# A fused Perceiver layer in f32: transposes among products, one more product ahead, another bank for the counts, and the last rows in two banks

## The chip, the core and the metric

The kernel runs on one core of a Trainium2 chip. The metric is the device time of one execution in microseconds (us), as the median of several runs. A profiled execution gives a trace beside it: every instruction of every engine with its start and its duration.

## What is computed

A tensor `x` of 8 x 64 rows of 512 numbers passes three blocks, each added to `x`, all in f32:

```
x = x + xattn(layernorm(x), ctx_1024, W, b)      # cross attention: 8 x 1601 context rows
x = x + attn(layernorm(x), wq, wk, wv, wo, ...)  # causal linear attention, 16 heads of 64, then an MLP with gelu
x = x + ffn(layernorm(x), w_router, w0, w1, wo)  # 8 experts, top 2 per row, gated by softmax
```

- `xattn`: scores of each row against all context rows, softmax, weighted sum, times `W`, relu.
- `attn`: its own layernorm, `q` and `k` through `elu(. @ proj) + 1`, `v = h @ wv`, running sums over the rows, `@ wo`, then layernorm and a hidden layer of 2048.
- `ffn`: the router picks two of eight experts for each row; each expert is `(silu(x @ w0) * (x @ w1)) @ wo`, and the two results are added with their weights.

## The kernel before

The 512 rows are four tiles of 128 (`NT = 4`), and the 512 features four chunks of 128 (`KC = 4`). All engines but the DMA queues run in the order in which the code is written. Loads of the context and of all weights come in one fixed order through a ring of twelve 1 MB buffers (`stream`, `need`), issued on SyncE's queue.

PSUM has eight banks of 512 columns. Up to the experts two rings of four are used: `mm_bank` for short results, and `acc_bank` for those that accumulate longer (or lie apart for another reason). For the experts both rings are closed (`banks.close()`) and a new pool `pse` is opened over the same eight banks, with `side_bank` (three for the whole tiles, two for the small groups) and `y_bank` (one bank for each of 0, 1 and "w"). A bank that comes around again, or that a pool takes over, makes its first writer wait for the readers of what lay there. Two engines that read one bank are put one after the other too: the second waits on a semaphore of the first.

The four places of the change, in the order of time:

1. Cross attention, around 160 to 178 us. The loop over tiles makes the attended rows of a tile (`attended`), and VectorE and ScalarE turn them into `hn` (`add_and_normalize`: two layernorms). `turn_h(t)` transposes `hn` on TensorE (line 552) and VectorE scales the four pieces into `h_t` (line 554). `values(t, n)` multiplies `h_t` of tile t with half n of `wv` (line 567), four products into one bank. After the loop stand the products of tile 2, the transposes of tile 3, and the products of tile 3.
2. The output projection of linear attention, around 252 to 290 us. `output(t, js)` adds the products of tile t for the pairs of heads j in `js` (line 758). The last pair, j = 7, comes from `attend_j(7)`: two groups of products (lines 712, 722), then on VectorE an addition (731), a reciprocal (732) and a product into `a_t` (734). Products for other j stand ahead of those that need j = 7. Then `join(t)` adds the result to `xin` and takes its statistics, `normal(t)` normalizes it, and `turn_h2(t)` transposes it for the MLP; the first hidden products (`hidden`, line 839) need these.
3. The border between routing and experts, around 403 to 410 us. `first_rows` gathers the rows of the first expert by products with one-hot matrices into two banks; ScalarE copies the one and VectorE the other into `xg_t0` (line 1110). One product with ones gives the experts' counts of rows (line 1107), and VectorE copies them (line 1112). The first expert's products (`up`, line 1243) read `xg_t0`.
4. The end, from 615 us. The last expert's tile, key (7, 0), goes through `whole_tile`: four `up` products into hidden quarters, each gated, transposed (`hidden_t`, line 1208), and multiplied by `down(q, h_t)` (line 1251) into one bank `y`. `add_rows` scales `y` by the gate, for this tile half on ScalarE (line 1218) and half on VectorE (line 1219), and GpSimd writes the rows to `out` by an indirect DMA that adds (line 1224).

Of the kernel before, what the change touches and what calls it, by code (L numbers as in the profile page):

```python
# [16 lines left out]
AF = mybir.ActivationFunctionType  # L17
# [16 lines left out]
NQ = 4  # L34
# [13 lines left out]
def perceiver_kernel(  # L48
# [35 lines left out]
    def mm_bank(name):  # L84
        return ps.tile([P, 512], F32, tag="mm", name=name)

    def acc_bank(name):
        return ps.tile([P, 512], F32, tag="acc", name=name)
# [460 lines left out]
    def turn_h(t):  # L549
        bank = mm_bank(f"tr_h_{t}")  # L550
        for c in range(KC):
            nc.tensor.transpose(bank[:, c * P : (c + 1) * P], hns[t][:, c * P : (c + 1) * P], ident)
        for c in range(KC):
            nc.vector.tensor_scalar(  # L554
                h_t[:, c, t * P : (t + 1) * P],
                bank[:, c * P : (c + 1) * P],
                g1_c[:, c : c + 1],
                beta1_c[:, c : c + 1],
                ALU.mult,
                ALU.add,  # L560
            )

    def values(t, n):
        wv_n = need("wv", n)
        bank = mm_bank(f"v_{n}_{t}")
        for c in range(KC):
            nc.tensor.matmul(  # L567
                bank, h_t[:, c, t * P : (t + 1) * P], wv_n[:, c, :], start=(c == 0), stop=(c == KC - 1)
            )
        nc.scalar.copy(v_sb[:, t, n * 512 : (n + 1) * 512], bank)  # L570
# [49 lines left out]
            values(t - 2, 1)  # L620
        attended(t)
    add_and_normalize(NT - 1)
    for n in range(2):
        values(NT - 2, n)
    turn_h(NT - 1)
    for n in range(2):
        values(NT - 1, n)
    done(("wv", 0), ("wv", 1))
# [6 lines left out]
    if True:  # L635
# [118 lines left out]
        def output(t, js):  # L754
            if t not in wo_banks:
                wo_banks[t] = (mm_bank if t < 2 else acc_bank)(f"wo_{t}")
            for j in js:
                nc.tensor.matmul(  # L758
                    wo_banks[t],
                    a_t[:, j, t * P : (t + 1) * P],  # L760
                    wo_r[j // 4][:, j % 4, :],
                    start=(j == 0),
                    stop=(j == nj - 1),
                )
# [8 lines left out]
        products(nj - 1)  # L773
        output(1, range(nj - 2))
        attend_j(nj - 1)
        output(2, range(nj // 2))
        for t in range(2):
            output(t, [nj - 2, nj - 1])

# [34 lines left out]
        of = join(0), join(1)  # L814
        for t in range(2):
            normal(t, *of[t])
        output(2, range(nj // 2, nj))
        of = join(2)
        output(3, range(nj // 2))
        normal(2, *of)  # L820
# [282 lines left out]
    count_tile(t)  # L1103
    first_rows(KC)

    bank = mm_bank("counts")
    nc.tensor.matmul(bank[:, :NE], ones, members[:, NT - 1, :], start=True, stop=True)
    xg_t0 = [moe.tile([P, 2, P], F32, name=f"xgT_first_{h}") for h in range(2)]
    for h, copy in enumerate([nc.scalar.copy, nc.vector.tensor_copy]):
# [31 lines left out]
    if True:  # L1141
# [5 lines left out]
        def y_bank(side, name):  # L1147
            return pse.tile([P, 512], F32, tag=f"y{side}", name=name)
# [64 lines left out]
        def add_rows(key, y, n, side, by_vector=False):  # L1213

            _, dst, gate = slots[key]
            y_sb = moe2.tile([P, D], F32, tag=f"ysb{side}", bufs=2 - side, name=f"y_sb_{key[0]}_{key[1]}")
            if key == (NE - 1, 0):
                nc.scalar.activation(y_sb[:n, : D // 2], y[:n, : D // 2], AF.Copy, scale=gate[:n, :])
                nc.vector.tensor_scalar(y_sb[:n, D // 2 :], y[:n, D // 2 :], gate[:n, :], None, ALU.mult)
            elif by_vector:  # L1220
                nc.vector.tensor_scalar(y_sb[:n, :], y[:n, :], gate[:n, :], None, ALU.mult)
            else:
                nc.scalar.activation(y_sb[:n, :], y[:n, :], AF.Copy, scale=gate[:n, :])  # L1223
            nc.gpsimd.indirect_dma_start(  # L1224
                out=out,
                out_offset=bass.IndirectOffsetOnAxis(ap=dst[:n, :], axis=0),
                in_=y_sb[:n, :],
                in_offset=None,
                bounds_check=B * S + P - 1,
                oob_is_err=True,  # L1230
                compute_op=ALU.add,
            )

        def whole_tile(key, up_of, down_of, between=lambda k: None, side=0):


            nm = f"{key[0]}_{key[1]}"
            xg_t = turned[key]

            def up(q):  # L1240
                bank = side_bank(side, f"up_{nm}_{q}")
                for c in range(KC):
                    nc.tensor.matmul(  # L1243
                        bank, xg_t[c], up_of[q][:, c, :], start=(c == 0), stop=(c == KC - 1)
                    )
                return gated(side, bank, f"{nm}_{q}")

            def down(q, h_t):
                w = down_of[q // 2]
                for j in range(2):  # L1250
                    nc.tensor.matmul(  # L1251
                        y, h_t[:, j, :], w[:, 2 * (q % 2) + j, :], start=(q + j == 0), stop=(q + j == NQ)
                    )

            hid0 = up(0)
            hid1 = up(1)
            h_t0 = hidden_t(side, hid0, f"{nm}_0")
            hid2 = up(2)
            y = y_bank(side, f"y_{nm}")
            down(0, h_t0)  # L1260
            h_t1 = hidden_t(side, hid1, f"{nm}_1")
            between(0)
            hid3 = up(3)
            h_t2 = hidden_t(side, hid2, f"{nm}_2")
            down(1, h_t1)
            between(1)
            h_t3 = hidden_t(side, hid3, f"{nm}_3")
            down(2, h_t2)
            between(2)
            down(3, h_t3)  # L1270
            add_rows(key, y, P, side)

        def group(e, up_of, down_of):


            nm = f"{e}_1"
            xg_t = turned[e, 1]


            split = "p (w n) -> p w n"  # L1280
            halves = [slice(h * P, (h + 1) * P) for h in range(2)]
            hid, h_t = [], {}

            def turn(j):
                bank = side_bank(1, f"ht_{nm}_{j}")
                nc.tensor.transpose(bank[:, :P], hid[j], ident)
                h_t[j] = moe2.tile([P, P], F32, tag="hidT1", name=f"hidT_{nm}_{j}")
                (nc.scalar.copy if j else nc.vector.tensor_copy)(h_t[j], bank[:, :P])

            for h in range(2):  # L1290

                bank = side_bank(1, f"up_{nm}_1") if h else y_bank(1, f"up_{nm}_0")
                for c in range(KC):

                    if h == 1 and c == KC - 1:
                        turn(0)
                    for q in range(NQ):
                        nc.tensor.matmul(
                            bank[q * R : (q + 1) * R, : 2 * P].rearrange(split, w=2),
                            xg_t[c],  # L1300
                            up_of[q][:, c, :].rearrange(split, w=2)[:, :, halves[h]],
                            start=(c == 0),
                            stop=(c == KC - 1),
                        )
                act = moe2.tile([P, P], F32, tag="act1", name=f"act_{nm}_{h}")
                nc.scalar.activation(act, bank[:, :P], AF.Silu)
                hid.append(moe2.tile([P, P], F32, tag="mid1", name=f"mid_{nm}_{h}"))
                nc.vector.tensor_tensor(hid[h], bank[:, P : 2 * P], act, ALU.mult)
            sums = {}

            def down(j, n):
                if j == 0:
                    sums[n] = y_bank(1, f"yq_{nm}_1") if n else side_bank(1, f"yq_{nm}_0")
                for q in range(NQ):
                    nc.tensor.matmul(
                        sums[n][q * R : (q + 1) * R, : D // 2],
                        h_t[j][:, q * R : (q + 1) * R],
                        down_of[q // 2][:, 2 * (q % 2) + j, n * D // 2 : (n + 1) * D // 2],
                        start=(j == 0),
                        stop=(j == 1),  # L1320
                    )

            down(0, 0)
            turn(1)
            down(0, 1)
            parts = []
            for n in range(2):
                down(1, n)
                parts.append(moe2.tile([P, D // 2], F32, tag="parts", name=f"parts_{nm}_{n}"))
                (nc.scalar.copy if n else nc.vector.tensor_copy)(parts[n], sums[n][:, : D // 2])  # L1330
            y = side_bank(1, f"y_{nm}")
            for n in range(2):
                nc.tensor.matmul(
                    y[:R, n * D // 2 : (n + 1) * D // 2], fold, parts[n], start=True, stop=True
                )
            add_rows((e, 1), y, R, 1)

        def three_groups(e, up_of, down_of):

# [67 lines left out]
            y = y_bank(1, f"y3_{nm}")  # L1407
            for g, n in [(0, 0), (1, 0), (2, 0), (0, 1), (1, 1), (2, 1)]:
                folded(g, n)
            add_rows((e, 1), y, REST, 1, by_vector=True)  # L1410

        if True:

# [314 lines left out]
```

## Time and profile before

| | us |
|---|---|
| median of three runs (650.0 to 650.8) | 650.71 |
| the profiled execution | 647.66 |
| its span, first to last instruction | 645.5 |
| TensorE busy in it | 620.4 |
| VectorE, ScalarE, GpSimd busy | 185.5, 127.8, 64.6 |

The stages by the trace: products run from about 7 us; the last wait of TensorE for a load is over at 121 us; linear attention begins at 177 us, the MLP's hidden layer at about 286, the experts' products at 409, and the last product ends before 637 us. The granted clock of TensorE was 0.996 of full speed on average.

How to read it: a line of the timeline gives start, duration, engine (PE is TensorE, PEld its weight loads, DVE VectorE, ACT ScalarE, POOL GpSimd), line of the kernel, operation, output <- inputs, shape, how many, and in brackets the idle time of the engine ahead of it and what ended that. The ends of products are modelled, so they overlap the next start by some 0.16 us; starts are the surer measure. The chain is the work that ended last, followed back from the end; its lines have start, duration, engine, output and line.

### The profile page before, as it was taken

Reading aid. Unit: us, or ns where it says so; the run is one execution under the profiler, and the core shown is the slowest. Engines: PE = TensorE matmul, PEld = TensorE weight load, DVE = VectorE, ACT = ScalarE, POOL = GpSimd, SP = SyncE. Lnnn points to the kernel's source line nnn. Section 1 sums busy time; section 2 is a strip of 40 time slices with the busy share of each in tenths; the row PEclk is TensorE's granted clock in tenths of the full one; section 3 lists DMA queues with packets and bytes.
Section 4 is the critical chain, followed back from the end, with each engine's and each line's share of the span. In section 5 each row is a group of like instructions: output and inputs, shape, how many; then the busy total and the mean of one; then the engine's idle time right before and its main releaser. Section 6 shows DMA issues by size and latency. Waiting matters only on the chain.

```text
span 645.5 us, 7558 instructions
## 1 busy us (share of the span) xinstructions
PE 620.4 (96%) x2956; PEld 292.7 (45%) x2956; DVE 185.5 (29%) x450; ACT 127.8 (20%) x245; POOL 64.6 (10%) x87
## 2 busy tenths in 40 slices
PE   4999999999999999999999999999999999999994
PEld 3743434344444444455444447544443344444441
DVE  5011333332316888660000035511311211011100
ACT  2241222220132123031101211311111111111110
POOL 4000000000000000050000002250102012103000
PEclk9999999999999999999999999999999999999998
DMA  8999999999421203030312222339392549496611
GB/s 345 405 414 422 423 425 421 427 426 422 193 80 47 86 2 131 1 131 0 130 52 79 70 96 95 134 95 348 114 375 54 200 206 338 173 367 188 274 18 16
DMA packets 23755, 132.70 MB, mean 206 GB/s; under 512 B 4084, under 2 KB 4084, under 8 KB 12184
## 3 DMA queue, kind: packets, MB, share of 16 engines
q1 hardware_dynamic: 19352, 123.37, 48.0%
q0 software_dynamic: 3248, 7.58, 5.3%
q10 hardware_dynamic: 1104, 1.07, 0.5%
q8 instruction: 33, 0.54, 0.3%
q14 instruction: 18, 0.15, 0.1%
HBM read 127.10 MB, written 4.91 MB: 204 GB/s over the span
## 4 chain that ended last, share of the span: by engine, by line
PE 50%; DMA 23%; issue 22%; DVE 2%; POOL 1%; POOLq 1%; ACT 0%; SPq 0%; ACTq 0%
DMA out_dram<-y_sb,dst_late 11%; DMA ctx<-in_ctx_dram 11%; PE hid L839 8%; PE mlp L860 8%; PE wk L647 4%; PE wq L647 4%; PE v L567 4%; PE wo L758 4%; PE sc L442 3%; PE av L503 3%; PE pw L380 3%; PE pr_wq L663 1%; PE xo L537 1%; PE qk L689 1%; POOL xg L1166 1%
## 5 line engine op out<-in xcount | busy, mean ns | idle before, releaser
L1243 PE MATMUL up<-e_up,xgT 128*128 128x512 f32 x224 | 100.2, 595 | 2.3 <-PEq L1569 1.4
L1243 PEld LDWEIGHTS up<-e_up,xgT 128*128 128x128 f32 x224 | 40.9, 190 | 49.9 <-issue 48.1
L1251 PE MATMUL y<-e_wo,hidT 128*128 128x512 f32 x128 | 60.8, 598 | 0.0
L839 PE MATMUL hid<-v_sb,w 128*128 128x512 f32 (+2 forms) x144 | 56.6, 545 | 0.0
L1202 DVE TENSOR_TENSOR mid<-up,act 128x256 f32<-128x256 f32 x35 | 14.9, 425 | 132.0 <-ACT act L1200 132.0
L860 PE MATMUL mlp<-w,hid_sb 128*128 128x512 f32 x112 | 51.0, 597 | 0.0
L503 PE MATMUL av<-ctx,eT 128*64 128x512 f32 x192 | 46.6, 597 | 0.7 <-DMA ctx<-in_ctx_dram 0.6
L442 PE MATMUL sc<-ctxT,pw_t 128*64 128x401 f32 (+1 forms) x256 | 46.2, 501 | 0.0
L839 PEld LDWEIGHTS hid<-v_sb,w 128*128 128x128 f32 x144 | 26.2, 190 | 29.1 <-issue 27.3
L1224 POOL DMA_INDIRECT out_dram<-y_sb,dst_late x12 | 18.3, 1524 | 174.3 <-ACT y_sb L1223 55.7
L1200 ACT ACTIVATE act<-up 128x256 f32<-128x256 f32 x35 | 13.4, 384 | 107.2 <-PE up L1243 97.4
L854 POOL TENSOR_TENSOR xin<-xin,b_bc 128x512 f32<-128x512 f32 x4 | 5.1, 1265 | 272.6 <-DVE rstd_h L796 268.4
L1251 PEld LDWEIGHTS y<-e_wo,hidT 128*128 128x128 f32 x128 | 22.5, 190 | 19.9 <-issue 19.6
L860 PEld LDWEIGHTS mlp<-w,hid_sb 128*128 128x128 f32 x112 | 20.7, 190 | 23.5 <-issue 23.4
L442 PEld LDWEIGHTS sc<-ctxT,pw_t 128*64 128x64 f32 x256 | 19.5, 136 | 25.6 <-issue 24.3
L758 PE MATMUL wo<-wo,a_t 128*128 128x512 f32 x64 | 29.1, 600 | 0.5 <-DVE a_t L734 0.5
L647 PE MATMUL wk<-h_t,wk 128*128 128x512 f32 x64 | 29.5, 604 | 0.0
L647 PE MATMUL wq<-h_t,wq 128*128 128x512 f32 x64 | 29.4, 602 | 0.0
L567 PE MATMUL v<-wv,h_t 128*128 128x512 f32 x64 | 28.7, 596 | 0.6 <-DVE h_t L554 0.6
L908 DVE TENSOR_TENSOR xs<-mlp,xs 128x512 f32<-128x512 f32 x3 | 2.1, 692 | 86.6 <-PE mlp L860 86.6
L732 DVE RECIPROCAL rden<-rden 128x512 f32<-128x512 f32 x8 | 26.8, 3353 | 0.3
L503 PEld LDWEIGHTS av<-ctx,eT 128*64 128x64 f32 x192 | 13.7, 136 | 26.8 <-issue 23.2
(266 smaller groups left out, 651.4 us busy)
## 6 DMA issues: line engine op xcount, KB each, us to landing
e_up<-in_L_ffn_up_dram SPq DMA_DIRECT2D x32, 1024.0 KB, 8.0
ctx<-in_ctx_dram SPq DMA_DIRECT2D x24, 1024.0 KB, 17.2
ctxT<-in_ctx_T_dram SPq DMA_DIRECT2D x24, 802.0 KB, 14.8
e_wo<-in_L_ffn_wo_dram SPq DMA_DIRECT2D x16, 1024.0 KB, 9.6
w<-in_L_attn_w_dram SPq DMA_DIRECT2D x8, 1024.0 KB, 4.7
ctxT<-in_ctx_T_dram SPq DMA_DIRECT2D x8, 796.0 KB, 17.5
wv<-in_L_attn_wv_dram SPq DMA_DIRECT2D x2, 1024.0 KB, 16.6
wq<-in_L_attn_wq_dram SPq DMA_DIRECT2D x2, 1024.0 KB, 17.8
```

Of the source, the lines that this page charges most:

```text
L380: nc.tensor.matmul(bank[:, : 2 * P], w_sb[:, oc, hc * P : (hc + 1) * P], p_t[:, oc, cols], start=(oc == 0), stop=(oc == KC - 1),)
L442: nc.tensor.matmul(sc[h * S : (h + 1) * S, :width], pw_t[:, c, (2 * t + h) * S : (2 * t + h + 1) * S], keys[h][:, c, :], start=(c == 0), s ...
L503: nc.tensor.matmul(av[h * S : (h + 1) * S, :], e_t[:, 4 * g + j, h * S : (h + 1) * S], rows[h][:, j, :], start=(g == 0 and j == 0), stop=F ...
L567: nc.tensor.matmul(bank, h_t[:, c, t * P : (t + 1) * P], wv_n[:, c, :], start=(c == 0), stop=(c == KC - 1))
L647: nc.tensor.matmul(bank, w[:, c, (j % 4) * P : (j % 4 + 1) * P], h_t[:, c, :], start=(c == 0), stop=(c == KC - 1),)
L732: nc.vector.reciprocal(rden, rden)
L758: nc.tensor.matmul(wo_banks[t], a_t[:, j, t * P : (t + 1) * P], wo_r[j // 4][:, j % 4, :], start=(j == 0), stop=(j == nj - 1),)
L839: nc.tensor.matmul(hid_banks[f][:, tokens], w[:, c, (f % 4) * P : (f % 4 + 1) * P], h2_t[:, c, tokens], start=(c == 0), stop=(c == KC - 1),)
L860: nc.tensor.matmul(acc[t], hid[:, t * P : (t + 1) * P], need("w2", f // 4)[:, f % 4, :], start=(f == 0), stop=(f == FF // P - 1),)
L1224: nc.gpsimd.indirect_dma_start(out=out, out_offset=bass.IndirectOffsetOnAxis(ap=dst[:n, :], axis=0), in_=y_sb[:n, :], in_offset=None, boun ...
L1243: nc.tensor.matmul(bank, xg_t[c], up_of[q][:, c, :], start=(c == 0), stop=(c == KC - 1))
L1251: nc.tensor.matmul(y, h_t[:, j, :], w[:, 2 * (q % 2) + j, :], start=(q + j == 0), stop=(q + j == NQ))
```

## The change

- The transposes of tile 3 (`turn_h(NT - 1)`) are issued inside the last group of products for v of tile 2, ahead of the fourth of its four products, instead of after the group.
- Five products of tile 2 (j = 0 to 4) instead of four stand ahead of the output products that need j = 6 and 7; the fifth is taken from those behind.
- The product for the counts gets a bank of the ring `acc` instead of `mm`.
- For the last expert's whole tile `y` is two banks, `y_bank(0)` and `y_bank("w")`, of 256 columns each. Each step of `down` makes its two products for the first bank and then its two for the second, with 256 columns each; ScalarE scales the first bank and VectorE the second. All other tiles keep one bank.

```
-    def values(t, n):
+    def values(t, n, among=lambda: None):
...
         for c in range(KC):
+            if c == KC - 1:
+                among()
             nc.tensor.matmul(
...
-    for n in range(2):
-        values(NT - 2, n)
-    turn_h(NT - 1)
+    values(NT - 2, 0)
+    values(NT - 2, 1, lambda: turn_h(NT - 1))
...
-        output(2, range(nj // 2))
+        output(2, range(nj // 2 + 1))
...
-        output(2, range(nj // 2, nj))
+        output(2, range(nj // 2 + 1, nj))
...
-    bank = mm_bank("counts")
+    bank = acc_bank("counts")
...
-            if key == (NE - 1, 0):
-                nc.scalar.activation(y_sb[:n, : D // 2], y[:n, : D // 2], AF.Copy, scale=gate[:n, :])
-                nc.vector.tensor_scalar(y_sb[:n, D // 2 :], y[:n, D // 2 :], gate[:n, :], None, ALU.mult)
+            if len(y) == 2:
+                nc.scalar.activation(y_sb[:n, : D // 2], y[0][:n, : D // 2], AF.Copy, scale=gate[:n, :])
+                nc.vector.tensor_scalar(y_sb[:n, D // 2 :], y[1][:n, : D // 2], gate[:n, :], None, ALU.mult)
...
-                for j in range(2):
-                    nc.tensor.matmul(
-                        y, h_t[:, j, :], w[:, 2 * (q % 2) + j, :], start=(q + j == 0), stop=(q + j == NQ)
-                    )
+                width = D // len(y)
+                for n, bank in enumerate(y):
+                    for j in range(2):
+                        nc.tensor.matmul(
+                            bank[:, :width],
+                            h_t[:, j, :],
+                            w[:, 2 * (q % 2) + j, n * width : (n + 1) * width],
+                            start=(q + j == 0),
+                            stop=(q + j == NQ),
+                        )
...
-            y = y_bank(side, f"y_{nm}")
+            y = [y_bank(side, f"y_{nm}")]
+            if key == (NE - 1, 0):
+
+                y.append(y_bank("w", f"y_{nm}_1"))
```

More of the change, by code (lines that the diff above doesn't have):

```diff
@@ L1216, in add_rows @@
             y_sb = moe2.tile([P, D], F32, tag=f"ysb{side}", bufs=2 - side, name=f"y_sb_{key[0]}_{key[1]}")
-            if key == (NE - 1, 0):
-                nc.scalar.activation(y_sb[:n, : D // 2], y[:n, : D // 2], AF.Copy, scale=gate[:n, :])
-                nc.vector.tensor_scalar(y_sb[:n, D // 2 :], y[:n, D // 2 :], gate[:n, :], None, ALU.mult)
+            if len(y) == 2:
+                nc.scalar.activation(y_sb[:n, : D // 2], y[0][:n, : D // 2], AF.Copy, scale=gate[:n, :])
+                nc.vector.tensor_scalar(y_sb[:n, D // 2 :], y[1][:n, : D // 2], gate[:n, :], None, ALU.mult)
             elif by_vector:
+                (y,) = y
                 nc.vector.tensor_scalar(y_sb[:n, :], y[:n, :], gate[:n, :], None, ALU.mult)
             else:
+                (y,) = y
                 nc.scalar.activation(y_sb[:n, :], y[:n, :], AF.Copy, scale=gate[:n, :])
@@ L1335, in group @@
                 )
-            add_rows((e, 1), y, R, 1)
+            add_rows((e, 1), [y], R, 1)
         def three_groups(e, up_of, down_of):
@@ L1409, in three_groups @@
                 folded(g, n)
-            add_rows((e, 1), y, REST, 1, by_vector=True)
+            add_rows((e, 1), [y], REST, 1, by_vector=True)
         if True:
```

## The prediction

> **What bounds the kernel now.** I read the page's table of busy time first, then TensorE's own list of waits, then the timeline around each place that the diff touches, and last the order of the instructions, with their waits, in the two built programs.
>
> From the page:
> ```profile
> PE 620.4 (96%) x2956; PEld 292.7 (45%) x2956; DVE 185.5 (29%) x450; ACT 127.8 (20%) x245; POOL 64.6 (10%) x87
> ```
> TensorE is busy for all but 25.1 us. Of these 8.5 us are the tail after its last product, and some 9 us the start; a change of this kind can only take what is left between. TensorE's waits (us in total, times, longest), cut to the places of the diff:
> ```profile
> PE v L567 <- DVE h_t L554: 0.6, 1, 0.6
> ...
> PE wo L758 <- DVE a_t L734: 0.5, 1, 0.5
> ...
> PE up L1243 <- issue: 0.5, 1, 0.5
> ```
> Three waits of half a microsecond, one at each of the first three edits. The fourth edit is at the tail. The waits are read from modelled ends of products, so I measure each place again by its starts.
>
> **The unit.** An f32 product shows as two records (passes) in the profile. Where TensorE runs without a gap, loads of weights for 512-column products stand 0.429 us apart (273.02, 273.45, 273.88 in the timeline): one pass is 0.429 us, one product 0.858 us. A 128x128 transpose of f32 is one pass of 0.11 us in the chain (four in 0.44).
>
> **Edit 1, the transposes of tile 3 among the products for v.** Timeline:
> ```profile
> 167.57 0.55 DVE L363 TENSOR_SCALAR hn<-xin,mv_h,rstd_h 128x512 f32<-128x512 f32 x1
> ...
> 169.15 0.60 PE L552 MATMUL tr_h<-ident,hn 128*128 128x128 f32 x4
> ...
> 169.78 1.36 DVE L554 TENSOR_SCALAR h_t<-tr_h,col 128x128 f32<-128x128 f32 x4 [1.67 <-PE tr_h L552]
> 170.31 0.30 PEld L567 LDWEIGHTS v<-wv,h_t 128*128 128x128 f32 x2 [0.80 <-ACT v_sb L570]
> 170.34 7.11 PE L567 MATMUL v<-wv,h_t 128*128 128x512 f32 x16 [0.59 <-DVE h_t L554]
> ```
> The reader sees four transposes, VectorE's scaling of the first, and only then the products that need it. From the first product at 162.28 to the first of wq at 177.28 are 15.00 us; in them lie 32 passes (13.73) and four transposes (0.44): 0.83 us are stall. After the change the transposes stand two passes (0.86 us) earlier, at 168.29, and those two passes cover VectorE. What is late next? hn is done at 168.12; a dependent weight load starts some 0.05 later (v_sb ends at 288.93, its load is at 288.98) and lasts 0.14, so the transposes start at about 168.31: 0.02 lost. VectorE starts its scaling 0.63 after the transposes start, as before: 168.94, first piece done at 169.34. TensorE's two cover passes end at 169.60, the weight load for the next product can start at about 169.47 and takes 0.19: up to 0.06 lost. The other three pieces follow each 0.32 us, under the 0.858 of a product. So **0.75 saved** (0.83 - 0.08); if hn came late by some tenth, that tenth would be lost, with the two cover passes queued behind it. At worst the gain is 0.5, at best 0.83. The bank of the products is assigned before the transposes' in either order, so no bank changes hands.
>
> **Edit 2, one output product more ahead.**
> ```profile
> 266.52 4.56 PE L758 MATMUL wo<-wo,a_t 128*128 128x512 f32 x10
> ...
> 270.82 0.76 DVE L734 TENSOR_TENSOR a_t<-nd,rden 128x256 f32<-128x256 f32 x2
> 271.63 0.30 PEld L758 LDWEIGHTS wo<-wo,a_t 128*128 128x128 f32 x2 [1.38 <-DVE a_t L734]
> 271.63 9.71 PE L758 MATMUL wo<-wo,a_t 128*128 128x512 f32 x22 [0.55 <-DVE a_t L734]
> ```
> Four products of tile 2 and one of j = 6 hide VectorE's reciprocal and not its end; the product with j = 7 waits. From 266.52 to the transposes at 281.18 are 14.66 us for 32 passes (13.73): 0.93 over. A stretch of six such passes between products of 64 columns, 252.89 to 255.66, takes 2.77 for 2.57, so 0.20 belongs to the entry: the stall is 0.73, by the load times 0.82; I take 0.77. One more product is 0.86 of cover. The weights of j = 7 would be loaded at 271.35 and still wait to 271.63, so 0.04 stays. **0.73 saved** (bounds 0.5 and 0.82).
>
> Does a later step give it back? The joins of tiles 0 and 1 on VectorE start 0.08 later, since j = 7 comes 0.08 later. VectorE's second normalization (1.59 us, beside GpSimd's addition) ends at 278.5 and the join of tile 2 at once after it; its result is needed by the transposes that now come at about 283.0, and is there at 281.3. The twelve scalings of transposed pieces on VectorE and ScalarE, 281.82 to 286.25, start about 0.5 earlier, and their last is needed 1.6 us after the hidden products start (fifth and sixth pass done), so that holds. The last join starts at 286.13 on TensorE's end and moves with it. If VectorE did hold this up, all of the gain would go.
>
> **Edit 3, the counts' bank.** Timeline:
> ```profile
> 408.08 0.37 ACT L1110 COPY xgT_first<-first_rows 128x256 f32<-128x256 f32 x1 [1.78 <-PE first_rows L999]
> ...
> 408.87 0.16 DVE L1112 COPY count<-counts 128x8 f32<-128x8 f32 x1
> ...
> 409.10 0.30 PEld L1243 LDWEIGHTS up<-e_up,xgT_first 128*128 128x128 f32 x2 [0.57 <-ACT xgT_first L1110]
> ```
> ScalarE's copy, the operand of the first expert product, is there at 408.45, but the product starts after VectorE's copy of the counts at 409.03. In the old program the counts lie in bank 0, which is also the first bank of the expert stage; in the new one they lie in bank 5. That reads as 0.55 gained. But in the built program of the new kernel that first product still waits for the same count of VectorE's instructions, the one that the copy of the counts completes: the new pool of banks waits for all of the old one. Nothing between moves. **I take 0**, with 0 and 0.55 as bounds (no instruction is added, so no loss).
>
> **Edit 4, the last rows in two banks.**
> ```profile
> 633.16 3.60 PE L1251 MATMUL y<-e_wo,hidT 128*128 128x512 f32 x8
> ...
> 636.80 0.47 ACT L1218 ACTIVATE y_sb<-y,xg 128x256 f32<-128x256 f32 x1 [3.01 <-PE y L1251]
> 637.31 0.48 DVE L1219 TENSOR_SCALAR y_sb<-y,xg 128x256 f32<-128x256 f32 x1 [4.93 <-ACT y_sb L1218]
> 638.07 1.55 POOL L1224 DMA_INDIRECT out_dram<-y_sb,dst_late x1 [20.76 <-DVE y_sb L1219]
> ```
> VectorE's half waits for ScalarE's, and the write on GpSimd for VectorE's. In the new program VectorE waits for TensorE instead. ScalarE's bank is complete four short passes (0.86 us) before the last product ends, so its 0.47 lies beside products, and VectorE starts at 636.80: 0.51 gained. The price: eight products of 512 columns become sixteen of 256, so 32 passes with a weight load (0.19 us) in each instead of 16. Here a rule speaks against it. The Trainium skill, TensorE: Matmul & The Clock Gate, section Back-to-back issue gap, says that in a stream of load and product pairs both set the spacing, and gives 81 ns at 128 columns where the isolated gap would be about 56: some 25 ns a pair. By it 32 passes would pay 0.8 us, and the edit would lose 0.3. The chain has the near row, passes of 256 columns in this kernel:
> ```profile
> 393.63 2.16 PE mlp L1063 x10
> ```
> 0.216 a pass against 0.2145 for half of 0.429: 32 times the difference is 0.05. In the second half of that tile six passes took 1.40 (0.233), among other work; at that rate it is 0.6. I take the undisturbed row, since this stretch is undisturbed too: **0.46 saved**, bounds -0.1 and 0.51. GpSimd's indirect write (1.55) and the 4.7 us to its landing stay.
>
> **Sum.** 0.75 + 0.73 + 0 + 0.46 = 1.94 us. The profiled execution, 647.66 us with a span of 645.5, would be 645.7 with a span of 643.6. The median of the runs lies 3.05 above the profiled time; the same difference gives 650.71 - 1.94 = 648.8, or 0.3% less. TensorE has no stall between these places that depends on absolute time (its waits for DMA end at 121 us), so the gains pass on.
>
> **The rivals.** (a) The counts' wait goes too: 648.2. For it, the bank does change; against it, the wait in the new program. Part of it would be met again by the transposes of gathered rows at 429, where a load waits 0.17 for the gather. Chance 0.08. (b) Half the gain: one of the three covers fails, either hn late at edit 1, VectorE's queue of joins at edit 2, or the short passes at edit 4: about 1.94 - 0.7 = 1.2 saved, 649.5. For it, edit 1 leaves only 0.17 us between hn and its use. Chance 0.27. (c) Slower: the weight loads of edit 4's short passes are exposed. Place, the last expert's 32 passes; price, up to 32 x 0.19 = 6.1 us, which would give 654.8; it passes the gains once each pass costs 0.06 more (1.94 / 32). Against it, the 0.216 a pass above. Chance 0.05. (d) The stalls were only followed by others that the trace hides and all of it comes back: 650.6. Chance 0.05. The likeliest, three stalls gone and the counts' not: 0.55.
>
> **The numbers.** 0.2% of 650.7 is 1.3 us, about what a measurement of this kernel can tell from no change. The likeliest case alone spans 648.4 to 649.3 by its bounds, and is faster nearly always, 0.52 of 0.55; (a) 0.08; of (b) 0.08 passes 1.3 us. So faster 0.68, slower 0.05 from (c) and 0.01 of (d), same 0.26. The range takes in (a) and most of (b): 647.8 to 650.1.
>
> **What would show it.** Right: at edit 1 the first pass of the last products of tile 3 follows the one before it within 0.5 us, and v to wq takes about 14.2; at edit 2 no wait of wo for a_t is listed, and the 32 passes take 13.9; at edit 3 the wait of 0.5 is still there, with VectorE's copy of the counts before it; at edit 4 ScalarE's half ends before TensorE does, and VectorE's half starts with TensorE's end. Wrong: edit 4's passes above 0.23 us, a wait of tr_h for hn, or a longer wait at the transposes of h2.

## The result, and the profile after

The changed kernel takes 649.15 us (median of 16 runs, 647.75 to 651.3) and the kernel before 650.75 (16 runs, 649.19 to 653.8). The ratio is 0.9974 with a 95% interval of 0.9963 to 0.9986: 1.7 us less, between 0.9 and 2.4 (the two medians differ by 1.6). The prediction was 1.94 less.

The profiled execution of the changed kernel goes the other way: 649.36 us with a span of 647.2, against 647.66 and 645.5 before. So the two traces are compared place by place first, and the rest of the span after that.

**Edit 1.** The timeline of the changed kernel, TensorE alone:

```profile
162.09 6.17 PE L569 MATMUL v<-wv,h_t 128*128 128x512 f32 x14
168.10 0.61 PE L552 MATMUL tr_h<-ident,hn 128*128 128x128 f32 x4
168.54 7.89 PE L569 MATMUL v<-wv,h_t 128*128 128x512 f32 x18
176.27 2.31 PE L648 MATMUL wq<-h_t,wq 128*128 128x512 f32 x5
```

The line of v carries no wait any more. From the first product for v to the first of wq it is 14.18 us, where it was 15.00: 0.82 gained. Fourteen passes of 0.429 end at 168.10, and the transposes start then: hn, done at 167.94, was in time.

**Edit 2.**

```profile
265.51 14.00 PE L759 MATMUL wo<-wo,a_t 128*128 128x512 f32 x32
...
279.35 1.04 PE L803 MATMUL tr_h<-ident,v_sb 128*128 128x128 f32 x8
...
287.16 0.66 PE L803 MATMUL tr_h<-ident,v_sb 128*128 128x128 f32 x4 [0.31 <-DVE v_sb L798]
```

The 32 output passes are one unbroken row now: 13.84 us to the transposes, 14.66 before, so 0.82 gained. Five products are just enough: the weights that need the last `a_t` are still loaded 0.28 us late (0.52 us of idle time ahead of them instead of 0.24), and the pass before them covers that:

```profile
270.62 0.34 PEld L759 LDWEIGHTS wo<-wo,a_t 128*128 128x128 f32 x2 [0.52 <-DVE a_t L735]
```

The wait of the last transposes for VectorE is 0.31 (0.32 before): the queue of joins takes nothing back.

**Edit 3.**

```profile
406.25 0.37 ACT L1112 COPY xgT_first<-first_rows 128x256 f32<-128x256 f32 x1 [1.78 <-PE first_rows L1000]
...
407.04 0.15 DVE L1114 COPY count<-counts 128x8 f32<-128x8 f32 x1
...
407.27 0.30 PEld L1247 LDWEIGHTS up<-e_up,xgT_first 128*128 128x128 f32 x2 [0.57 <-ACT xgT_first L1112]
```

The wait is still 0.57, and the load still starts some 0.08 after the end of the counts' copy. Nothing moved.

**Edit 4.**

```profile
635.01 3.62 PE L1257 MATMUL y<-e_wo,hidT 128*128 128x256 f32 x16
...
637.80 0.47 ACT L1220 ACTIVATE y_sb<-y,xg 128x256 f32<-128x256 f32 x1 [2.17 <-PE y L1257]
638.67 0.48 DVE L1221 TENSOR_SCALAR y_sb<-y,xg 128x256 f32<-128x256 f32 x1 [4.45 <-PE y L1257]
639.92 1.55 POOL L1228 DMA_INDIRECT out_dram<-y_sb,dst_late  x1 [20.79 <-DVE y_sb L1221]
```

ScalarE's half ends before the products do and VectorE's starts with their end, as forecast. From the last tile's first product (616.87) to the last one's end it is 21.76 us, 21.72 before, so the short passes cost 0.04. VectorE's half ends 22.28 after that first product instead of 22.75. But GpSimd's write starts 0.77 after VectorE's end, where it was 0.28: 23.05 us from the first product, 23.03 before. **The half microsecond is won on VectorE and lost again on GpSimd.**

The chain at the end of the changed kernel (start, duration, what; POOLq is GpSimd's sequencer):

```profile
638.67 0.49 DVE y_sb L1221
639.16 0.03 POOLq L1228
639.19 0.51 issue
639.70 1.77 POOLq L1737
```

And of the kernel before:

```profile
637.83 1.78 POOLq L1724
```

A separate short instruction of GpSimd's sequencer, and 0.51 us of issue, stand between VectorE's end and the write. Before, the write's own work began at once, 0.04 after VectorE's end (637.79). The two programs say why. In both the write carries one wait itself, and its other waits stand in event instructions ahead of it (short instructions that only wait), one or two in each. The last of these and the write, with what each waits for:

```
before   ... event [DMA, DMA]     write [VectorE]
after    ... event [DMA, VectorE] write [ScalarE]
```

The write now depends on both engines. VectorE's wait, the last to be met, went into the event instruction, and the write holds ScalarE's, met long before.

**The rest of the span.** By these places the changed kernel is ahead by 1.83 us from the output projection up to the first expert product (407.30, 409.13 before; 0.19 of it arose ahead of the first edit). At the last expert's first product it is behind by 1.83 (616.87, 615.04). The 3.66 us between lie mostly in the experts 0, 3 and 5 (0.69, 1.14 and 1.62), whose small groups of rows stand in branches; experts 2 and 6 take 42.29 and 23.29 in both. The traces under "The expert stage" below show that experts 3 and 5 differ by as much between two executions of one kernel.

### The profile page after: what moved, and what is told of

It reads as the page before. It is cut to its first block, busy times and chain, and to the rows that moved or that the text cites. A ratio compares the mean times of both kernels' runs of the same rounds, so it can differ in the third digit from the quotient of the medians.

```text
span 647.2 us, 7591 instructions
## 1 busy us (share of the span) xinstructions
PE 619.2 (96%) x2972; PEld 294.6 (46%) x2972; DVE 185.4 (29%) x450; ACT 127.8 (20%) x245; POOL 64.6 (10%) x87
## 5 line engine op out<-in xcount | busy, mean ns | idle before, releaser
L1257 PE MATMUL y<-e_wo,hidT 128*128 128x512 f32 (+1 forms) x144 | 60.8, 550 | 0.0
L1257 PEld LDWEIGHTS y<-e_wo,hidT 128*128 128x128 f32 x144 | 25.5, 190 | 18.2 <-issue 17.2
```

The source lines that it names most:

```text
L1257: nc.tensor.matmul(bank[:, :width], h_t[:, j, :], w[:, 2 * (q % 2) + j, n * width : (n + 1) * width], start=(q + j == 0), stop=(q + j == NQ),)
```

## The experiments

Every ratio is to the kernel before on the same chip, with its 95% interval. The kernels were timed in batches, with the kernel before in each: its median was 647.49 us with e1, e2, e4 and e5, 650.41 with e3, e6, e7 and e8, and 650.7 with e9, e10 and e11. So only ratios and places in the trace are compared. "By place" means by the starts of instructions at the place of an edit. By its places the full change should be at 1 - 1.62/650 = 0.9975.

**e1_transposes_alone.** The first edit by itself.

```
+    def values(t, n, among=lambda: None):
...
+    values(NT - 2, 1, lambda: turn_h(NT - 1))
```

> Only the first edit (the transposes of tile 3 among the products for v). Theory: the stall between the first product for v of tile 2 and the first of wq goes as in the full change, from 15.0 us to 14.2, and everything behind moves by that: 0.8 us less in all, 0.1%. Rival, that the stalls only make room for others behind: the stretch is 14.2 and the output projection or the hidden layer starts no earlier; no change in all.

Measured: 0.9982 (0.9974 to 0.9991). From v (161.94) to wq (176.12) it takes 14.18 us. The output projection keeps its stall of 0.55, and its products after the stall start at 270.47 instead of 271.63:

```profile
270.47 9.71 PE L759 MATMUL wo<-wo,a_t 128*128 128x512 f32 x22 [0.55 <-DVE a_t L735]
```

Of these 1.16 us 0.34 were there ahead of the edit (v starts at 161.94, not 162.28); the other 0.82 are the edit's. They pass on to the output projection, and the rival falls.

**e2_product_alone.** The second edit by itself.

```
-        output(2, range(nj // 2))
+        output(2, range(nj // 2 + 1))
...
-        output(2, range(nj // 2, nj))
+        output(2, range(nj // 2 + 1, nj))
```

> Only the second edit (a fifth output product of tile 2 ahead). Theory: from the first of the last 32 output passes to the transposes for the MLP it takes 13.8 us instead of 14.7, the first hidden products and the last transposes of h2 come 0.8 earlier, 0.8 us less in all. Rival, that VectorE's queue of joins gives it back: the wait for the last normalization grows from 0.3 to about 1.1 and the hidden products of the last tile start where they did.

Measured: 0.9992 (0.9983 to 1.0001). In the trace v still waits (0.60), the 32 output passes take 13.83, and the last transposes of h2 wait 0.32. By place the 0.8 is there, and the ratio to expect from it, 0.9987, lies in the interval; the time alone would not tell it from no change.

**e4_last_rows_in_one_bank.** The full change without its fourth edit.

```
-            if len(y) == 2:
...
+            if key == (NE - 1, 0):
+                (y,) = y
...
-            if key == (NE - 1, 0):
-
-                y.append(y_bank("w", f"y_{nm}_1"))
```

> The full change with its fourth edit undone (the last rows in one bank again). Theory, that the two banks bring nothing because GpSimd starts its write 0.5 us later after VectorE's end: from the last tile's first product to GpSimd's write 23.03 us as before, and the time of the full change, 0.9974 of before. Rival, that the fourth edit brings its 0.46: 23.0 here but half a microsecond more in all than the full change.

Measured: 0.998 (0.9971 to 0.9989), and 23.03 us from the last tile's first product to the write. With or without the two banks the time agrees within the intervals.

**e5_engines_swapped.** The full change, and the two scalings of the last rows change engines.

```
-   nc.scalar.activation(y_sb[:n, : D // 2], y[0][:n, : D // 2], AF.Copy, scale=gate[:n, :])
-   nc.vector.tensor_scalar(y_sb[:n, D // 2 :], y[1][:n, : D // 2], gate[:n, :], None, ALU.mult)
+   nc.vector.tensor_scalar(y_sb[:n, : D // 2], y[0][:n, : D // 2], gate[:n, :], None, ALU.mult)
+   nc.scalar.activation(y_sb[:n, D // 2 :], y[1][:n, : D // 2], AF.Copy, scale=gate[:n, :])
```

The waits in the program are those of the full change: an event with VectorE's, the write with ScalarE's. Only which of the two comes last is turned around.

> The full change with the two scalings of the last rows swapped: VectorE takes the first bank, ScalarE the second. GpSimd's write then waits in an instruction of its own for VectorE, whose half is done early, and in the write itself for ScalarE, which is last. Theory, that the half microsecond is paid because the last event releases a separate wait ahead of the write: the gap from the end of the last half to GpSimd's write falls from 0.77 to about 0.28, and from the last tile's first product to the write it takes 22.55 us instead of 23.05; half a microsecond less than the full change. Rival, that any write that waits for two engines pays it: gap 0.77 and 23.05 as in the full change.

Measured: 0.9958 (0.9946 to 0.9971). Timeline and chain of the end:

```profile
613.46 7.11 PE L1247 MATMUL up<-e_up,xgT 128*128 128x512 f32 x16 [0.30 <-PEq L1627]
...
635.26 0.47 ACT L1221 ACTIVATE y_sb<-y,xg 128x256 f32<-128x256 f32 x1 [3.03 <-PE y L1257]
636.01 1.55 POOL L1228 DMA_INDIRECT out_dram<-y_sb,dst_late  x1 [20.28 <-ACT y_sb L1221]
```

```profile
634.40 0.49 DVE y_sb L1220
634.89 0.03 POOLq L1228
634.92 0.85 issue
635.78 1.79 POOLq L1737
```

From 613.46 to 636.01 are 22.55 us, and the gap after the last half (635.73) is 0.28. The event is passed at 634.92, while TensorE still works; the half microsecond after it is over by the time ScalarE ends, and the write goes on 0.05 after that. The rival, that any write with two engines pays 0.77, falls.

**e6_vector_scales_both.** The full change; VectorE scales both halves.

```
-   nc.scalar.activation(y_sb[:n, : D // 2], y[0][:n, : D // 2], AF.Copy, scale=gate[:n, :])
+   nc.vector.tensor_scalar(y_sb[:n, : D // 2], y[0][:n, : D // 2], gate[:n, :], None, ALU.mult)
```

> The full change with both halves of the last rows scaled by VectorE, one after the other, each from its bank; ScalarE has none. GpSimd's write then waits for VectorE alone, in the write itself. Theory of the separate wait: gap 0.28 from VectorE's end to the write, 22.55 us from the last tile's first product to the write. Rival, that the gap of 0.77 belongs to the two banks or to chance: 0.77 and 23.05.

Measured: 0.9957 (0.9944 to 0.9971); 22.56 us from the first product (616.86) to the write:

```profile
639.42 1.55 POOL L1228 DMA_INDIRECT out_dram<-y_sb,dst_late  x1 [20.29 <-DVE y_sb L1221]
```

VectorE's second half ends at 639.14. Two banks and one engine: gap 0.28. So the 0.77 belongs neither to the two banks nor to VectorE, but to the order of the two waits. All thirteen traces agree: the gap is 0.77 in the five whose write waits last in an event (the full change twice, e3, e7, e8) and 0.28 in the other eight.

**e3_count_copied_late.** The full change; the copy of the counts comes after the small instructions of the tables.

```
-    nc.vector.tensor_copy(count, bank[:, :NE])
     write(NT - 1)
     for t in range(NT - 2, NT):
         tabulate(t)
+    nc.vector.tensor_copy(count, bank[:, :NE])
```

> The full change, and VectorE's copy of the counts is moved behind the two tables' work (some 2.2 us of small instructions). Theory, that the first expert product waits for every reader of the old pool of banks, whichever bank the counts lie in: it starts 2 us later after ScalarE's copy, a wait of about 2.7 instead of 0.57, and the time is about 2 us more than that of the full change. Rival, that only the bank counts, which is now another: the product starts at once after the two copies of the gathered rows, no later than in the full change.

Measured: 1.0029 (1.0018 to 1.0039).

```profile
406.59 0.42 DVE L1112 COPY xgT_first<-first_rows 128x256 f32<-128x256 f32 x1 [1.09 <-PE first_rows L1000]
...
409.40 0.16 DVE L1117 COPY count<-counts 128x8 f32<-128x8 f32 x1
...
409.63 0.30 PEld L1247 LDWEIGHTS up<-e_up,xgT_first 128*128 128x128 f32 x2 [3.05 <-issue]
```

Both operands were there at 407.01; the product waited for the copy of the counts, from a bank that is not its own. The wait grew from 0.57 to 3.05, somewhat more than the 2.7 expected. In all the kernel is some 3.5 us above the full change (1.0029 against 0.9974), where the wait grew by 2.5. The profile shows a second cost right behind the wait. The first products of expert 0 in the full change, and then here, with the granted clock of this trace in tenths (40 slices of 16.2 us; 9 is 90% or more, and the first 8 is the slice from 405.8):

```profile
407.30 7.11 PE L1247 MATMUL up<-e_up,xgT_first 128*128 128x512 f32 x16 [0.51 <-issue]
```

```profile
409.67 8.80 PE L1247 MATMUL up<-e_up,xgT_first 128*128 128x512 f32 x16 [2.99 <-issue]
...
PEclk9999999999999999999999999899999999999998
```

The same sixteen passes take 1.69 us longer. From 410.9 to 414.3 the granted clock is 0.51 of full speed, and the weight loads there stand 0.85 us apart instead of 0.43. No other of the thirteen traces shows a clock below full speed between 20 and 635 us, and none has so long a wait of TensorE there. By place that is 2.5 + 1.7 = 4.2 us, which the intervals leave room for. The twenty runs of this kernel agree: their granted clock is 0.990 to 0.995, 0.993 on average, where the kernel before beside them has 0.993 to 0.998, 0.996 on average.

**e9_counts_early_swapped.** The swapped kernel, with product and copy of the counts ahead of VectorE's copy of the rows.

```
-    first_rows(KC)
...
+    first_rows(2)
...
     bank = acc_bank("counts")
     nc.tensor.matmul(bank[:, :NE], ones, members[:, NT - 1, :], start=True, stop=True)
+    first_rows(2)
+    count = moe.tile([P, NE], F32, name="count")
+    nc.vector.tensor_copy(count, bank[:, :NE])
...
-    count = moe.tile([P, NE], F32, name="count")
-    nc.vector.tensor_copy(count, bank[:, :NE])
```

> The full change with the engines of the last rows swapped, and the product for the counts and VectorE's copy of them two products earlier, ahead of the copies of the gathered rows. If the first expert product waits for all readers of the old pool, it now ends with VectorE's copy of the gathered rows: the wait falls only from 0.57 to about 0.5, and in all this is the time of the swapped kernel. If it waited for the counts' copy alone, it would start right after ScalarE's copy, half a microsecond earlier.

Measured: 0.9964 (0.9951 to 0.9978).

```profile
406.38 0.17 DVE L1111 COPY count<-counts 128x8 f32<-128x8 f32 x1 [0.77 <-PE counts L1108]
...
406.93 0.42 DVE L1114 COPY xgT_first<-first_rows 128x256 f32<-128x256 f32 x1 [0.38 <-PE first_rows L1000]
...
407.43 0.30 PEld L1247 LDWEIGHTS up<-e_up,xgT_first 128*128 128x128 f32 x2 [0.73 <-issue]
```

ScalarE's copy ends at 406.63. With the counts copied by 406.55, the product waits for the next reader of the old pool, VectorE's copy of the second half of the rows (done 407.35), though its first two chunks need the first half alone. The wait did not shrink to 0.5 as expected but grew to 0.73: the counts' product, now among the last products of the rows, puts that copy off.

**e7_transposes_earlier.** The full change; the transposes one product earlier.

```
-            if c == KC - 1:
+            if c == KC - 2:
```

> The full change with the transposes of tile 3 ahead of the third product instead of the fourth. Theory, that hn comes only just in time for the fourth: the transposes wait about 0.8 us for hn, with two products behind them, and from the first product for v of tile 2 to wq it takes 15.0 us again; the first edit's gain is gone. Rival, that the order among the products matters little: 14.2 as in the full change.

Measured: 0.9983 (0.9972 to 0.9995). From v (161.94) to wq (176.99) 15.05 us.

```profile
167.94 0.63 PE L552 MATMUL tr_h<-ident,hn 128*128 128x128 f32 x4 [0.68 <-DVE hn L363]
```

hn is done at 167.80, and the gain of the first edit is gone. So the place of the edit is not free by a whole product: at the fourth product hn is just in time, at the third it is not.

**e8_two_products_ahead.** The full change; six products of tile 2 ahead instead of five.

```
-        output(2, range(nj // 2 + 1))
+        output(2, range(nj // 2 + 2))
...
-        output(2, range(nj // 2 + 1, nj))
+        output(2, range(nj // 2 + 2, nj))
```

> The full change with six products of tile 2 ahead instead of five. Theory: nothing is left to cover, since a_t is just in time with five; the joins start 0.86 us later, VectorE's queue holds the last join back by about 0.5, and the wait of the last transposes of h2 grows from 0.3 to about 0.8: about 0.5 more than the full change. Rival, that VectorE's queue has room: the stretch and the wait stay as in the full change.

Measured: 0.9979 (0.9966 to 0.9991).

```profile
287.62 0.66 PE L803 MATMUL tr_h<-ident,v_sb 128*128 128x128 f32 x4 [0.83 <-DVE v_sb L798]
```

The output passes take 13.84 as with five, and the last transposes wait 0.83 instead of 0.31: VectorE starts the last join at 284.77, where it was 284.30 in the full change, though the hidden products ahead of the wait start at the same time (284.05 and 284.10): VectorE's queue is now behind. This is the give-back that the prediction asked about; it starts with the sixth product, not with the fifth. The time cannot show half a microsecond.

**e10_change_again and e11_swapped_again**, on one chip.

> The full change once more, beside the swapped one on the same chip: 0.9974 to 0.998 of before, 1.6 us less; gap of 0.77 before GpSimd's last write. Its profile also tells how much the small groups' part of the expert stage differs between executions of one program: theory, by up to some 3 us, with no relation to the change.

> The swapped kernel once more, on the same chip as the full change: by the theory half a microsecond (0.0008) below it, so about 0.997; a rival that the swap brings a whole microsecond or more elsewhere, as 0.9958 of its first timing might say, would put it 0.0016 below.

Measured: 0.9959 (0.9947 to 0.9971, 6 runs) and 0.9964 (0.9954 to 0.9973, 21 runs). By place the one takes 23.05 us from the first product (616.94) to the write (639.99), the other 22.55 (615.64 to 638.19), as in their first traces. In time they can't be told apart, so neither the half microsecond nor a larger effect of the swap is shown by time. The 0.9959 of the repeated change lies below what its places give, 0.9975, by more than its own interval, and below its first timing of 0.9974, though these two intervals overlap; why is open.

**The expert stage.** From the first product of expert 0 to that of expert 7, by the starts of their first products, in us, with the median of the kernel before in the same batch:

| kernel | kernel before | expert 0 | 3 | 5 | all seven |
|---|---|---|---|---|---|
| before | 650.71 | 31.69 | 30.86 | 30.86 | 205.91 |
| full change | 650.75 | 32.38 | 32.00 | 32.48 | 209.57 |
| full change again | 650.7 | 32.02 | 31.99 | 32.50 | 209.32 |
| e1 | 647.49 | 30.86 | 30.86 | 30.86 | 205.27 |
| e5, swapped | 647.49 | 32.22 | 30.86 | 30.86 | 206.29 |
| e11, swapped again | 650.7 | 31.10 | 32.01 | 32.47 | 208.34 |

One kernel, the swapped one, takes 206.29 and 208.34. The largest differences sit in the experts 0, 3 and 5, whose small groups take the branch of line 1298 before (1311 now); the experts 1 and 4 differ by up to 0.5, while expert 2 takes 42.28 or 42.29 in all thirteen traces and expert 6 23.29 or 23.30.

Experts 3 and 5 take two values each, and these go with the batch rather than with the kernel. In the four traces of the first batch (e1, e2, e4, e5) both take 30.86 us (once 30.95); in the eight traces of the full change, e3 and e6 to e11 expert 3 takes 31.9 to 32.0 and expert 5 32.3 to 32.5. The swapped kernel, with all four edits, is on both sides. The kernel before was itself some 3 us faster in the first batch. Its one trace, with 30.86 in both, is of an execution of 647.66 us, as in the first batch and 3.05 below the median of its own runs. So the two profiles at the top compare a short expert stage with a long one, and 2.76 of the 3.66 us are these two experts. No kernel without the fourth edit was traced in a later batch, so that it too takes the longer times there is read from its median alone. Where it arises, in expert 3 of the kernel before and of the full change:

```profile
534.86 0.33 PE L1286 MATMUL ht<-ident,mid 128*128 128x128 f32 x1 [0.34 <-DVE mid L1308]
```

```profile
535.15 0.33 PE L1299 MATMUL ht<-ident,mid 128*128 128x128 f32 x1 [1.21 <-DVE mid L1321]
```

TensorE waits for VectorE up to 1.2 us in these groups of the changed kernel's trace and up to 0.3 in that of the kernel before. What sets the batches apart is open; whether fetching of instructions behind a branch has to do with it was not tried.

## Why the prediction was right, and where not

- **Edit 1, predicted 0.75, measured 0.82.** The step that hn at 168.12 would be just in time for 168.29 held (167.94 and 168.10 in the new trace), and e7 shows the edge. The 0.08 allowed for two late weight loads was nearly all unspent.
- **Edit 2, predicted 0.73, measured 0.82.** The 0.20 that I put down to the entry from products of 64 columns was too much: with no stall the 32 passes take 0.11 above 13.73. By the starts of the weight loads I had 0.82; that was the better reading. The steps on VectorE held: nothing is given back with five products, and e8 shows that it begins with six.
- **Edit 3, predicted 0, measured 0.** The bank changed and the wait did not. e3 shows that the first product waits for the counts' copy out of another bank, and e9 that it waits for the readers of the old pool together.
- **Edit 4, predicted 0.46, measured -0.02. This step failed.** The half on VectorE went as forecast (22.28 instead of 22.75 us after the last tile's first product), and so did the price of the short passes: 0.04, where I had 0.05 from the near row and the rule for pairs of load and product gave 0.8. What failed is the sentence "GpSimd's indirect write (1.55) and the 4.7 us to its landing stay". I saw that VectorE now waits for TensorE, and did not ask what the write waits for. It got a second engine to wait for, and VectorE's wait moved into an event instruction ahead of it: 0.51 us of issue that had been hidden lay after the last event. The Trainium skill, Perfetto Trace Analysis, section Identifying Dependency Chains, says that instructions waiting on several engines may get such event instructions ahead of them; it gives no price, and e5 and e6 measure it here: 0.49.
- **The sum.** 0.82 + 0.82 + 0 - 0.02 = 1.62 instead of 1.94, near the 1.7 (0.9 to 2.4) of the ratio. Part of that nearness is luck: edits 1 and 2 brought 0.16 more than I had, which hides a third of the 0.48 missing at edit 4. It is the rival of half the gain in its kind, one of the covers failing, at edit 4; but through a wait that I had not listed, where the rival named the short passes, and with five sixths of the gain kept.

By place the best version is the full change with the engines swapped: 0.82 + 0.82 + 0.48 = 2.1 us. Both of its timings lie below the kernel before, 0.9958 and 0.9964; that it beats the full change is shown at the place only.

## What to carry to other kernels

When a dependency between two engines is cut, look at who waits for both: a consumer that had one engine to wait for now has two, and one of the waits moves into an instruction ahead of it. Let the engine that is last be the one whose wait the consumer itself carries, or let one engine do both parts.

To fill a stall with independent products, fit the cover to the stall on both sides: here one product behind the transposes, and one more ahead of the output products, were right. A second product ahead only delayed the next engine's queue, and transposes one product earlier stalled on their own operand. Another bank frees nothing where a whole pool is handed over at once.

## What the runs showed of the hardware

- On GpSimd, 0.51 us of issue lies between a passed event instruction and the indirect write behind it; it runs on while the write waits for another event (e5: event passed at 634.92, write's work at 635.78, 0.05 after ScalarE's end).
- Passes of 256 columns with a weight load in each, 0.19 us long, run as closely as passes of 512 in f32: eight output products cost 0.04 us more as 32 passes than as 16.
- After a wait of 3.05 us TensorE's granted clock was 0.51 for 3.4 us, and the passes behind it cost 1.7 us more (e3). The waits of up to 1.4 us in the other traces are followed by no such dip.
- Experts 3 and 5, with small groups behind branches, take 1.1 and 1.6 us more in one execution of the swapped kernel than in another, while two other experts repeat within 0.01. This goes with the batch rather than with the kernel; the cause is open.
